# The second modulation and the attention's weights moved behind batch 0's first product, with the written order kept on all engines from there on

## The chip, the cores and the metric

The kernel runs on one core of a Trainium2 chip. The time is device time of one launch in microseconds (us), from the first to the last work of the core. A core has five engines that run side by side, each working through its own queue in order: TensorE (PE in the profile: matrix products and transposes, with PEld for the loading of the stationary operand), VectorE (DVE), ScalarE (ACT), GpSimd (POOL) and SyncE (SP, which here only issues DMA transfers). An instruction that waits for another engine holds back everything that stands behind it in its own queue. So the order in which instructions stand in each queue is part of the kernel.

## What is computed

The reference is a network of two layers on `x` of 8 batches x 512 positions x 128 channels. Each layer has two halves, and before each half the activations are normalised, scaled and shifted by a modulation that is computed from a conditioning vector of the batch:

```python
mod = (silu(c) @ wmod).reshape(8, 6, 1, 128)       # one such mod for each layer
sa, ca, ga, sb, cb, gb = mod[:, 0], ..., mod[:, 5]
ga = (2 * (ga >= 0) - 1) * maximum(abs(ga), 0.25)  # gb likewise
h = layernorm(x) * (1 + ca) + sa
x = x + ga * attn(h)
h = layernorm(x) * (1 + cb) + sb
x = x + gb * ffn(h)
```

In layer 0, `attn` is a recurrence over time (exponentials and running sums of products k, v and r, then a division, then a product with `Wo`), and `ffn` is a linear layer whose inputs and weights are rounded to a 6-bit grid in blocks of 32. In layer 1, `attn` is an attention of 16 heads with three branches (latent keys, 32 chosen positions, window keys), gated and summed, and `ffn` is a gated recurrence over the batches.

## The kernel before

Everything is kept with 128 channels or positions on the partitions and the 512 positions of one batch along the free dimension, in 32-bit floats, so most instructions are 128x512.

Three chains of work are written as Python generators: `layer0()` (for each batch, `layer0_mix` and then `layer0_linear`), `before()` (for each batch, `prepare`, which makes layer 1's inputs) and `recurrence()`. Each `yield` is a place where other work can be put between. The attention's loop (from line 968) walks over 192 units of scores, softmax and weighted sums, and calls `advance`, which takes one step of each chain where the loop leaves room. So while batch b is in the attention, layer 0 of a later batch goes on between the pieces. Before that loop there is nothing to attend to: batch 0 has to go through `layer0_mix`, `layer0_linear`, `prepare` and `group_inputs` first. That stretch is called the start here.

The start is recorded like this. The loads are issued, `modulate(0)` makes layer 0's modulation (line 239; six small products on PE, line 226, called modps, and then small DVE instructions), the mixing weights are scaled (lines 241 to 249), and then

```python
FIRST = 14
for _ in range(FIRST):
    next(stages[0])
remaining()
```

takes 14 steps of `layer0()` and records `remaining()`: the second modulation (`modulate(1)`, line 253), the quantised weight of layer 0's linear half (`mx_quantize` of `fw`, lines 256 to 265, with a transpose on PE called wps), the scaling of the attention's weights on DVE (lines 267 to 276) and the mask on POOL (lines 278 to 281). After that `while (0, 0) not in q_of: next(feed)` and `need("shared", 0)` (lines 955 to 957) record the rest of the start.

The recording is not yet the order in the queues. A scheduler orders the instructions of each engine by what it takes to be urgent, unless they stand inside `tc.manual_schedule(...)`, where the named engines keep the written order. In the kernel before, that region is opened just ahead of the attention's loop (lines 966 and 967), so the start is in the scheduler's order and the attention in the written one.

Names that the change touches, in the order of batch 0's path: `xn` (normalised input, L118), `tp` (its transpose, L126), `h` (L311), products `wkT`, `wvT`, `wrT` (L315, L316), `k` and `v` (L321, L324), `er` (exponential of r, L327), the maximum scan `mx` (L332), `d` and `q` (L335 to L340), their exponentials (L342 to L356), the running sums `aa` (L360, L364) and `bb` (L368), numerator and denominator (L363 to L377), reciprocals (L381), their product `v` (L383), the product `o` with `Wo` (L386), `oT` (L388), the residual (`rp` L131, `x` L133). Then the linear half ends in a second residual, and `prepare` makes `xn1`, `tp1`, `hT` (L442), the latents `cps` and `cq` (L449, L451), their squares and reciprocal roots `ss` and `rr` (L456 to L461, L91 to L96), `tpq` (transposed `cq`), `nqT` (L475), and from it `qR`, `qN`, `k0N`, `k1R` and the first scores `s` (L793). Layer 0 of batch 1 (its `xn`, `tp`, `h`, `wkT` to `wrT`, `k`, `v`, `er`, `mx`, `d`, `q`) is woven into this stretch.

Of the kernel before, what the change touches and what calls it, by code (L numbers as in the profile page):

```python
# [58 lines left out]
def adaln_kernel(ctx: ExitStack, tc: tile.TileContext, x, pa, pb, pc, pt, out):  # L59
    nc = tc.nc  # L60
    V, S, G, PE = nc.vector, nc.scalar, nc.gpsimd, nc.tensor
# [73 lines left out]
    def mx_quantize(dst, src, nb, tmp, key):  # L135

        am = small.tile([128, nb], FP, name=f"am_{key}", tag="am")
        V.tensor_reduce(am, src, AX.X, ALU.max, apply_absolute_value=True)
        yield 0
        sc = small.tile([128, nb], FP, name=f"sc_{key}", tag="sc")  # L140
        V.tensor_scalar(sc, am, 1.0 / 7.5, 1e-30, ALU.mult, ALU.max)
        rc = small.tile([128, nb], FP, name=f"rc_{key}", tag="rc")
        V.reciprocal(rc, sc)
        z = tmp("z")
        V.tensor_tensor(z, src, rc.unsqueeze(2).to_broadcast([128, nb, 32]), ALU.mult)

        yield 0
        e = tmp("e")  # L150
        V.tensor_scalar(e.bitcast(U32), z.bitcast(U32), 0x7F800000, None, ALU.bitwise_and)
        yield 0
        m1 = tmp("m1")
        V.tensor_scalar(m1, e, 1.0, 1.5 * 2.0**20, ALU.max, ALU.mult)
        m2 = tmp("m2")
        V.tensor_scalar(m2, e, 1.0, 1.5 * 2.0**20 + 0.125, ALU.max, ALU.mult)
        q2 = tmp("q2")
        G.tensor_tensor(q2, z, m2, ALU.add)
        yield 0
        q1 = tmp("q1")  # L160
        V.tensor_tensor(q1, z, m1, ALU.add)
        G.tensor_tensor(q2, q2, m2, ALU.subtract)
        yield 0
        V.tensor_tensor(q1, q1, m1, ALU.subtract)
        yield 0
        V.tensor_tensor(q1, q1, q2, ALU.min)
        yield 0
        V.tensor_tensor(dst, q1, sc.unsqueeze(2).to_broadcast([128, nb, 32]), ALU.mult)
# [22 lines left out]
    def bank(shape, name):  # L191
        return ps_t.tile(shape, FP, name=name, tag="t")
# [5 lines left out]
    def part(n, *shape, rows=128):  # L198
        nonlocal taken
        taken += n  # L200
        ap = room[0:rows, taken - n : taken]
        return ap.rearrange("p (a b) -> p a b", b=shape[-1]) if shape else ap
# [13 lines left out]
    def modulate(l):  # L216
        c_in = WA[f"cT{l}"]

        sg = part(B)
        S.activation(sg, c_in, AF.Tanh, scale=0.5)  # L220
        si = sil0 if l == 0 else part(B)
        V.tensor_scalar(sg, sg, 0.5, 0.5, ALU.mult, ALU.add)
        V.tensor_tensor(si, sg, c_in, ALU.mult)
        ps = bank([128, 6, B], f"modps{l}")
        for j in range(6):
            PE.matmul(ps[:, j, :], lhsT=WA[f"wmod{l}"][:, j * 128 : (j + 1) * 128], rhs=si, start=True, stop=True)
        m = mods[l]
        V.tensor_copy(m, ps)
        for j in (1, 4):
            V.tensor_scalar(m[:, j, :], m[:, j, :], 1.0, None, ALU.add)  # L230
        for j in (2, 5):
            sgn = part(B)
            V.tensor_scalar(sgn, m[:, j, :], 0.0, 2.0, ALU.is_ge, ALU.mult)
            mag = part(B)
            V.scalar_tensor_tensor(mag, m[:, j, :], -1.0, m[:, j, :], ALU.mult, ALU.max)
            V.tensor_scalar(mag, mag, 0.25, None, ALU.max)
            V.scalar_tensor_tensor(m[:, j, :], sgn, -1.0, mag, ALU.add, ALU.mult)
# [12 lines left out]

    def remaining():

        modulate(1)


        wq = part(128, 4, 32)
        for _ in mx_quantize(
            wq, WA["fw"].rearrange("p (n k) -> p n k", k=32), 4,
            lambda n: part(128, 4, 32), "w",
        ):  # L260
            pass
        wps = bank([128, 128], "wps")
        PE.transpose(wps, wq.rearrange("p n k -> p (n k)"), ident)
        S.copy(wqT, wps)
        V.tensor_scalar(gbias, mod0[:, 5, :], WA["fbias"], None, ALU.mult)

        qscale = 1.0 / math.sqrt(HD)
        gq = part(1, rows=QL)
        V.tensor_scalar(gq, WB["g"][0:QL, :], qscale, None, ALU.mult)
        V.tensor_scalar(wd[0:QL, :], wd[0:QL, :], gq, None, ALU.mult)  # L270
        V.tensor_scalar(wd[QL:128, 0:512], wd[QL:128, 0:512], WB["g"][QL:128, :], None, ALU.mult)
        V.tensor_scalar(WB["wdk"][0:KVL, :], WB["wdk"][0:KVL, :], WB["g4"][0:KVL, :], None, ALU.mult)
        V.tensor_scalar(WB["wkr"], WB["wkr"], 1.0 / H, None, ALU.mult)

        for n in ("ufT", "uiT", "ucT", "uoT", "bf", "bi"):
            V.tensor_scalar(WC[n], WC[n], 0.5, None, ALU.mult)

        G.memset(mask, 0.0)
        G.affine_select(
            mask, mask, pattern=[[-1, T]], compare_op=ALU.is_ge, fill=NEG, base=T - 128, channel_multiplier=1  # L280
        )
# [603 lines left out]
    def layer0():  # L885
        for b in range(B):
            while b > 3 and ("normed", b - 2) not in ready or b == 1 and ("normed", 0) not in ready:
                yield 0
            yield from layer0_mix(b)
            yield from layer0_linear(b)  # L890
            ready.add(("layer0", b))

    def before():
        for b in range(B):
            while ("layer0", b) not in ready or b > 1 and ("attended", b - 2) not in ready:
                yield 0
            while b > 2 and ("recur", b - 3) not in ready:
                yield 0
            yield from prepare(b)

    def recurrence():
        for b in range(B):
            while ("attended", b) not in ready or (b < B - 2 and ("normed", b + 2) not in ready):
                yield 0
            yield from recur(b)
            ready.add(("recur", b))

    FIRST = 14
    stages = layer0(), before(), recurrence()
    chains = {chain: 0 for chain in stages}  # L910
    for _ in range(FIRST):
        next(stages[0])
    remaining()

    def advance(open_to=TR, of=None):

        for chain in of or list(chains):
            if chains[chain] % M > 0:
                chains[chain] -= 1
            elif chains[chain] in (0, TR, open_to):  # L920
                gap = next(chain, None)
                if gap is None:
                    del chains[chain]
                else:
                    chains[chain] = gap
# [37 lines left out]
    FEEDS = (1, 1, 2, 1, 2, 2)  # L963
    late = []
    projecting = None
    ordered = ExitStack()
    ordered.enter_context(tc.manual_schedule(engines={PE.engine, V.engine, S.engine, G.engine}))
    for i in range(-2, len(units) + 3):
        un = units[i] if 0 <= i < len(units) else None
        ahead = units[i + 2] if i + 2 < len(units) else None  # L970
# [159 lines left out]
```

## Time and profile before

| | before |
|---|---|
| median of 3 runs | 1708.04 us (1707.66 to 1712.55) |
| profiled execution | 1708.48 us, its span 1706.7 us |
| PE busy | 1572.7 us (92% of the span) |
| DVE busy | 1266.0 us (74%) |
| ACT busy | 1152.8 us (68%) |
| POOL busy | 936.8 us (55%) |
| first product of the attention's scores starts | 94.81 us |
| PE busy from 96 us to 1706 us | 1531.83 us of 1610 |
| PE busy from 24 us to 96 us | 27.7 us of 72 |

The table is read in two parts. From 96 us on the PE is busy for 95% of the time, and the instructions of every engine stand in an order that the change leaves as it is. The first 96 us are the start, in which one batch passes from engine to engine, and PE is busy for little more than a third of the time from 24 us on. The column PEclk of the profile gives the clock that TensorE was granted, as a share of full speed: 0.50 means that a product takes about twice as long.

### The profile page before, as it was taken

The numbers are of one execution on the slowest core, as the hardware profiler recorded it, in microseconds if no ns is written. First come the engines' busy times: TensorE is split into PE (matmuls) and PEld (weight loads), VectorE is DVE, ScalarE is ACT, GpSimd is POOL, SyncE is SP. The second block draws the span as 40 slices with busy tenths as digits, with TensorE's granted clock in tenths as the row PEclk, the third lists the DMA queues.
The fourth block names the chain that finished last, engine by engine and source line by source line (L and its number), as shares of the span: only waits on it lengthen the run. The fifth ranks groups of instructions, "written<-read, shape, count | busy, mean of one in ns | idle before, by whom it ended". The sixth has DMA issues, their size and how long they took to land.

```text
span 1706.7 us, 39939 instructions
## 1 busy us (share of the span) xinstructions
PE 1572.7 (92%) x14777; PEld 938.1 (55%) x14777; DVE 1266.0 (74%) x4259; ACT 1152.8 (68%) x3245; POOL 936.8 (55%) x1370
## 2 busy tenths in 40 slices
PE   3388999899999999999899999989999999999997
PEld 2144655465555655655555555655555565665663
DVE  6678878875888868975979768867889667666543
ACT  2244787666776777777666677767776777777882
POOL 2155567554666547554656457654666456655551
PEclk8687999998999999999999999999999999999998
DMA  4000000000000000000000000000000000000012
GB/s 170 1 2 2 2 2 3 7 2 14 3 2 8 7 8 3 1 8 14 3 1 2 7 8 3 2 7 14 3 2 1 14 8 3 1 14 8 14 39 68
DMA packets 13778, 20.55 MB, mean 12 GB/s; under 512 B 912, under 2 KB 9104, under 8 KB 13456
## 3 DMA queue, kind: packets, MB, share of 16 engines
q1 hardware_dynamic: 13584, 17.99, 3.1%
q8 instruction: 118, 1.93, 0.5%
q14 instruction: 76, 0.62, 0.1%
HBM read 11.70 MB, written 5.77 MB: 10 GB/s over the span
## 4 chain that ended last, share of the span: by engine, by line
PE 63%; DVE 26%; ACT 5%; issue 3%; POOL 3%; DMA 0%; POOLq 0%; DVEq 0%; ACTq 0%
PE s L793 19%; PE t L837 12%; DVE p L805 7%; PE o L851 7%; PE s L755 2%; PE k3Rm L638 2%; PE qRm L638 2%; ACT p L814 2%; PE k3Np L610 1%; PE v1p L651 1%; PE op L862 1%; PE o L738 1%; PE qNp L610 1%; ACT pT L603 1%; POOL p L823 1%
## 5 line engine op out<-in xcount | busy, mean ns | idle before, releaser
L823 POOL TENSOR_SCALAR p<-p,rs 128x512 f32<-128x512 f32 (+3 forms) x1024 | 578.8, 586 | 390.9 <-DVE rs L819 221.9
L805 DVE CUSTOM_DVE_ANT_0 p<-s,mask 128x512 f32<-128x512 f32 (+3 forms) x1024 | 442.6, 477 | 178.4 <-PE s L793 178.0
L814 ACT ACTIVATE p<-p,nm 128x512 f32<-128x512 f32 (+3 forms) x1024 | 560.0, 553 | 11.9 <-DVE nm L805 11.8
L603 ACT COPY pT<-t 128x384 f32<-128x384 f32 (+1 forms) x768 | 354.8, 521 | 188.0 <-PE t L837 185.4
L837 PE MATMUL t<-ident,p 128*128 128x128 f32 x2560 | 367.4, 281 | 34.8 <-ACT pT L603 7.2
L837 PEld LDWEIGHTS t<-ident,p 128*128 128x128 f32 x2560 | 276.2, 142 | 160.3 <-issue 115.0
L814 ACT ACTIVATION_READ_ACCUMULATOR p<-p,nm 128x1 f32 x1024 | 197.2, 193 | 0.0
L793 PE MATMUL s<-k3R,qR 32*128 32x128 f32 (+3 forms) x2048 | 188.1, 458 | 4.4 <-DVE nm L805 3.2
L793 PE MATMUL s<-k1R,qR 32*128 32x512 f32 (+3 forms) x2048 | 185.9, 452 | 2.6 <-POOL k1R L625 2.5
L851 PE MATMUL o<-pT,v 128*32 128x512 f32 (+3 forms) x2048 | 153.2, 440 | 0.0
L793 PEld LDWEIGHTS s<-k3R,qR 32*128 32x128 f32 x2048 | 98.8, 188 | 84.4 <-DVE nm L805 30.9
L793 PEld LDWEIGHTS s<-k1R,qR 32*128 32x128 f32 x2048 | 105.4, 186 | 48.5 <-issue 13.6
L851 PEld LDWEIGHTS o<-pT,v 128*32 128x32 f32 x2048 | 60.4, 110 | 111.1 <-issue 100.3
L793 PE MATMUL s<-k0N,qN 32*128 32x512 f32 (+3 forms) x1024 | 102.3, 434 | 0.0
L793 PE MATMUL s<-k3N,qN 32*128 32x512 f32 (+3 forms) x1024 | 96.8, 434 | 0.0
L625 POOL TENSOR_TENSOR k3R<-k3R,rt_k3R 128x512 f32<-128x512 f32 x32 | 40.7, 1272 | 83.9 <-DVE rt_k3R L624 83.9
L805 DVE DVE_READ_ACCUMULATOR2_ANT nm<- 128x1 f32 x1024 | 82.8, 81 | 0.1
L765 POOL TENSOR_TENSOR p<-p,m 128x512 f32<-128x512 f32 x32 | 33.6, 1049 | 67.4 <-DVE m L764 67.4
L638 PE MATMUL qRm<-nqT,wb 96*128 96x512 f32 x128 | 68.8, 621 | 1.2 <-ACT nqT L475 0.7
L793 PEld LDWEIGHTS s<-k0N,qN 32*128 32x128 f32 x1024 | 60.5, 188 | 17.0 <-issue 2.5
L793 PEld LDWEIGHTS s<-k3N,qN 32*128 32x128 f32 x1024 | 55.1, 189 | 22.1 <-issue 15.2
L603 ACT COPY accT<-o 128x512 f32<-128x512 f32 x32 | 18.8, 587 | 71.0 <-PE o L851 71.0
(308 smaller groups left out, 2446.3 us busy)
## 6 DMA issues: line engine op xcount, KB each, us to landing
wb<-pb_dram SPq DMA_DIRECT2D x1, 3731.0 KB, 14.3
x<-x_dram SPq DMA_DIRECT2D x8, 256.0 KB, 3.7
x1all<-x SPq DMA_DIRECT2D x7, 256.0 KB, 2.0
h2all<-h SPq DMA_DIRECT2D x7, 256.0 KB, 2.0
h2o<-h2all SPq DMA_DIRECT2D x7, 256.0 KB, 2.6
x_first<-x1all SPq DMA_DIRECT2D x4, 256.0 KB, 3.6
out_dram<-x_first SPq DMA_DIRECT2D x4, 256.0 KB, 2.2
out_dram<-x SPq DMA_DIRECT2D x4, 256.0 KB, 2.3
```

The source lines that it names most:

```text
L603: S.copy(dst, src)
L610: PE.matmul(ps, lhsT=w[:, g * 128 : (g + 1) * 128], rhs=src, start=True, stop=True)
L625: G.tensor_tensor(lo, lo, r[0], ALU.subtract)
L638: PE.matmul(ps, lhsT=w[:, i * 128 : (i + 1) * 128], rhs=src, start=True, stop=True)
L755: PE.matmul(sp[h][to, :], lhsT=k[js, g, :], rhs=q[js, h * half : (h + 1) * half], start=(i == 0), stop=(i == 2), skip_group_check=True,)
L765: G.tensor_tensor(p2, p2, m2.unsqueeze(2).to_broadcast([128, T // 32, KEEP]), ALU.subtract)
L793: PE.matmul(un.s[j][:, at : at + n], lhsT=q[js, n - 128 : n], rhs=k[js, 0:n], start=(i == 0 and at == 0), stop=(i == 2), skip_group_check= ...
L805: V.tensor_tensor_reduce(out=un.p[:, j, at : at + n], in0=un.s[j][:, at : at + n], in1=mask[:, T - n :], scale=-1.0, scalar=3.4e38, op0=AL ...
L814: S.activation(p, p, AF.Exp, bias=un.nm[:, j, i : i + 1], scale=-1.0, accum_out=un.rs[:, j, i : i + 1])
L823: G.tensor_scalar(p, p, un.rs[:, j, i : i + 1], 1.0, ALU.mult, ALU.mult)
L837: PE.transpose(tp[:, k, :], un.p[:, j, at : at + 128], ident)
L851: PE.matmul(out_ps[js, c * 128 :], lhsT=v[:, c, js], rhs=pT[:, j, at[0] : at[-1] + 1 : step, :], start=not a and c == 0, stop=False, skip_ ...
```

## The change

The second modulation and the scaling of the attention's weights, the recurrent weights and the mask go from `remaining()` into a function of their own, `remaining_later()`. `remaining()` keeps the quantised weight and its bias. The written order begins earlier: the region `tc.manual_schedule` opens before the first steps of `layer0()`. In it, 10 steps are recorded, then `remaining()`, then 21 more steps (up to the product of numerator and reciprocals, just ahead of the product `o`), then `remaining_later()`, and then the rest of the start as before.

```diff
     def remaining():
 
-        modulate(1)
-
 
         wq = part(128, 4, 32)
...
         S.copy(wqT, wps)
         V.tensor_scalar(gbias, mod0[:, 5, :], WA["fbias"], None, ALU.mult)
 
+    def remaining_later():
+
+        modulate(1)
         qscale = 1.0 / math.sqrt(HD)
         gq = part(1, rows=QL)
...
-    FIRST = 14
+    SECOND = 21
+    FIRST = 10
     stages = layer0(), before(), recurrence()
     chains = {chain: 0 for chain in stages}
+    ordered = ExitStack()
+    ordered.enter_context(tc.manual_schedule(engines={PE.engine, V.engine, S.engine, G.engine}))
     for _ in range(FIRST):
         next(stages[0])
     remaining()
+    for _ in range(SECOND):
+        next(stages[0])
+    remaining_later()
...
-    ordered = ExitStack()
-    ordered.enter_context(tc.manual_schedule(engines={PE.engine, V.engine, S.engine, G.engine}))
     for i in range(-2, len(units) + 3):
```

What this does to the queues, read from the two built programs (no times are in this): nothing is added and nothing is taken away. The DMA queue of SP keeps its order. On PE, ACT, POOL and DVE the order differs only ahead of the first softmax of the attention, and from there on it is the same, instruction by instruction. Inside the start:

- PE: wps moves ahead of `wrT`; the six products modps of the second modulation stay directly in front of `o`.
- ACT: `er` moves ahead of the exponentials of batch 0; the tanh of the second modulation moves behind them. For batch 1, `er` and then `nqT`, `qN` and `k0N` stand ahead of its exponentials, which came first before.
- DVE: seven instructions of the quantised weight and of the second modulation's input leave the stretch ahead of `xn`. The second modulation's input (L222, L223) now stands directly behind the product of numerator and reciprocals, and the rest of the modulation and the scaled weights follow it, ahead of the residual `x`. In batch 0's first residual block, L363 moves ahead of the running sum `bb`. In `prepare`, batch 1's normalisation, which alternated with batch 0's one instruction by one, follows it as a block, ahead of `ss`; and batch 1's `mx`, `d` and `q`, which stood inside `rr`, move behind it, with `d` and `q` between the rotations of `qR` and `k1R`.
- POOL: the mask moves behind the numerator of batch 0 (L372); batch 1's `d` moves between the rotations of `qR` and of `k1R`.

## The prediction

> **What bounds the kernel now.** I read the page's engine table and slices first, then the chain of work that ended last for the first 120 us, then the timeline of the same stretch, and last the windows, for the clock. From 96 us on PE is busy for 1531.83 of 1610 us and no queue's order changes there. So the change can only move the moment at which the first scores start, and what it moves goes to the end one to one: behind that moment DVE (37.73 of the 42 us from 96 to 138) and then PE have no gap to take a delay in. The chain of work, time order (start, length, what):
>
> ```profile
> 14.79 2.08 PE wkT L315 x2
> ...
> 23.21 1.24 PE modps L226 x12
> 24.45 0.17 PE wps L263
> 24.62 14.30 issue
> 38.92 2.06 PE o L386 x2
> 41.00 0.70 ACT oT L388
> 41.74 1.13 PE rp L131 x4
> 42.89 0.70 DVE x L133
> ...
> 83.51 0.67 PE tpq L126 x4
> 84.20 0.59 ACT nqT L475
> ...
> 96.03 3.68 PE s L793 x16
> ```
>
> One batch is handed from engine to engine. The "issue" of 14.30 us is no issue: PE's queue holds `o`, which needs DVE's product at 38.13. The timeline shows what ACT, POOL and DVE do meanwhile:
>
> ```profile
> 22.01 0.63 ACT L342 ACTIVATE d<-d 128x512 f32<-128x512 f32 x1
> ...
> 23.77 0.58 ACT L327 ACTIVATE er<-wrT 128x512 f32<-128x512 f32 x1
> ...
> 25.57 1.55 POOL L364 TENSOR_TENSOR aa<-aa,e 128x512 f32<-128x512 f32 x1 [2.13 <-ACT e L351]
> 25.99 1.24 DVE L230 TENSOR_SCALAR mod<-mod 128x8 f32<-128x8 f32 x2
> 26.08 0.63 ACT L356 ACTIVATE q<-q 128x512 f32<-128x512 f32 x1
> 27.14 0.16 DVE L233 TENSOR_SCALAR start<-mod 128x8 f32<-128x8 f32 x1
> ...
> 28.52 1.02 DVE L270 TENSOR_SCALAR wb<-wb,start 96x1536 f32<-96x1536 f32 x1
> ...
> 38.13 0.69 DVE L383 TENSOR_TENSOR v<-v,e 128x512 f32<-128x512 f32 x1
> ```
>
> The second modulation and the weights sit on DVE inside the chain. And two small L230 last 1.24 us, to the end of POOL's L364 at 27.12: DVE stands while POOL reads. The clock, by windows (us, PE busy, ..., granted clock third from the end):
>
> ```profile
> 75.00:75.50 0.50, 0.26 (x2) 0.00 (x0) 0.00 (x0) 0.23 (x2) 0.39 (x1) 0.53 0.00 0
> 85.50:86.00 0.50, 0.50 (x3) 0.18 (x2) 0.00 (x0) 0.00 (x0) 0.00 (x0) 0.72 0.00 0
> 95.50:96.00 0.50, 0.45 (x7) 0.00 (x0) 0.00 (x0) 0.00 (x0) 0.48 (x1) 0.95 0.00 0
> 99.00:99.50 0.50, 0.50 (x4) 0.00 (x0) 0.00 (x0) 0.00 (x0) 0.00 (x0) 0.63 0.00 0
> ```
>
> It flips between half and full about 75.5, 85.7, 96.0 and 99.4, distances of nearly three times, three times and once 3.4 us.
>
> **The change, step by step**, on the clock of the profiled execution (1708.48 us, span 1706.7; 0.44 above the median). No DMA moves, and what is moved needs only loads that have landed by 24 us (the windows show DMA share 0 from there).
>
> 1. Ahead of `xn`: L138 leaves ahead of the first modulation (0.20 from its start to the next), L145 (0.20) and L151 (0.14) behind it. `wkT` starts at 14.79 - 0.5 = 14.3. The quantised weight then runs from 13 to 16, while DVE would wait for `k` until 18 ("DVE mx waited for ACT k", 3.8 us): free, as long as `k` is not earlier than 16.
> 2. PE: 0.5 us earlier at half clock is 0.25 at full clock, wps (0.17 to 0.3) now stands ahead of `wrT`: end 23.1 (23.2 before).
> 3. ACT: `er` stands ahead of the exponentials and waits for `wrT`. Before, `d` started at 22.01; now `er` at 23.1 and `d` at 23.65. From `d` to the end of the last exponential (26.71) it took 4.70 with `er` and wqT inside, some 3.7 without: 27.4 instead of 26.7.
> 4. DVE: L363, now ahead of `bb`, waits for that: 27.4; POOL's L364 (its running sum ends at 26.2) holds until 27.6, as it held L230. L363 ends 28.2, `bb` (1.22) 29.4. Then L371 needs `bb`, DVE has a gap, and POOL's L372 (1.27 alone, as at 120.24) gets in: L371 at 30.7. L551 and L374 to 32.3, L377 to 33.0, four reciprocals (34.64 to 38.13: 3.49) to 36.5. So L383 starts at 36.5 instead of 38.13: 1.6 won of the 3.9 us of modulation and weights that left (L228 0.18, L230 0.14, 27.14 to 30.06, L276 0.67). Without POOL's turn in between it is 35.3; with two DVE operations held as at 30.87 (POOL 3.18 there) 37.1.
> 5. The added wait: L222 and L223 stand behind L383, so modps starts at 36.5 + 0.6 + 0.4 = 37.5. PE is at half clock there (0.50 from 28 to 75), so the twelve take the 2.73 of 8.09, not the 1.24 of 23.21; and `o` stands behind them in PE's queue: 37.5 + 2.64 = 40.1 instead of 38.92, **+1.2**.
> 6. DVE's queue: behind modps (40.25) come the copy, eleven small ones (0.07 apart, 0.20 where one needs the last: 1.5), the weights (L270 0.94, L271 0.44, L272 0.40, L273 0.20) and L276 (0.67): 4.3 us, to 44.6. From `o` to `x` PE and ACT need 3.97 (38.92 to 42.89): 44.1. So this cover is 0.5 too short and `x` waits for DVE's queue, not for `rp`: 44.6, **+1.7**. The mask on POOL (0.53 + 0.61) fits behind L372, long before 96.
> 7. The linear half is unchanged: second residual 64.85 + 1.7 = 66.55.
> 8. `prepare`: batch 0's normalisation is no longer mixed with batch 1's. Residual to `xn1` took 4.97 (64.85 to 69.82); unmixed, the same block at 42.89 to 47.57 took 4.68. `xn1` 71.2, `hT` 72.9 to 73.7. Batch 1's block then starts when DVE is free, at 72.3: sums 1.2, then `hsum` waits for `hT` (73.7 + 0.6), and L91 to L118 take 2.56 (45.01 to 47.57): its `xn` runs 76.9 to 78.0, where it ended at 73.53. Tp and `h` (1.17, 0.79) put `wkT` of batch 1 at 79.4 instead of 76.13: **+3.3**.
> 9. PE's queue again: `tpq` stands behind `wrT` of batch 1. The DVE side improves: `ss` at 78.0, the root without `mx`, `d` and `q` inside 2.6 instead of 5.47 (77.17 to 82.64), `cq` ready at 82.5 instead of 83.45. But the six products end later than that. At full clock they take 5.4 (76.13 to 81.55): 84.8. At the clock of batch 0, whose lead-up is the same (tp, `h`, products, cold), 8.4 (14.79 to 23.21): 87.8. The clock rose 6.1 us into that run; with flips on a grid of 3.4 us it rises between some 2.8 and 6.2 us after the start, so I take 7.5: `tpq` at 86.9 instead of 83.51, **+3.4**.
> 10. `nqT` to the scores: 11.2 before (84.79 to 96.03). DVE's `d` and `q` (0.6 each) and POOL's `d` (1.27) now lie between the rotations; in exchange the products from 85.7 to 89.1, at half clock before, follow a busy stretch and run fast (1.8 us). By the rows I get 10.7 where DVE gets its turn between POOL's instructions and 12.5 where it does not; I take 11.0, **-0.2**.
>
> Sum: scores at 96.03 + 3.2. 1708.48 + 3.2 - 0.44 = **1711.2 us**, 0.19% more. Ends: 35.3 in step 4 (-1.25), full clock in step 9 (-2.1) and 10.7 in step 10 (-0.3) leave -0.4; 37.1 (+0.6), 87.8 (+0.9) and 12.5 (+1.5) give +6.2.
>
> [...]
>
> **The rivals.** *Slower, beyond 0.3%* (5.1 us, about what a measurement of this kernel can tell from no change): PE's queue with the clock. If the six products of batch 1 run at half clock to the end, they take 12 x 0.857 + 0.2 = 10.5, `tpq` comes at 89.9, +6.4, and the time is 1714.2; with step 10 at 12.5 it is 1715.7. It decides from `tpq` at 88.8 on. For it: 76% busy between 13.9 and 17.3 did not raise the clock. Against: it did rise at 20.9 and at 75.5 under such work.
>
> *Nothing arrives*: batch 1's tp gets to PE early enough, the products run at full clock, POOL keeps out of step 4. Then the start is -0.4 to +1: 1707.6 to 1709. For it: DVE has 3.9 us less ahead of `o`. Against: all of step 5 and 6 has to be paid from 1.6 us.
>
> *Faster*: the written order frees the root in step 9 (1 us) and L383 (1.6 to 2.9), and nothing stands behind PE's two queues. Even all together is 3.9 us: 1704. Beyond 0.3% faster it needs scatter as well; the runs before spread over 4.9 us.
>
> **How the numbers follow.** Forecast (+1 to +5.1) 0.50; nothing arrives 0.16; slower beyond 0.3% 0.28; faster 0.06. Within 0.3%: 0.50 + 0.16 = 0.66. The range takes the lower end less a little scatter, 1706.5, and the upper end of the sum plus some, 1715.7; half of the slow rival lies in it.
>
> **What would show it.** In the changed kernel: L383 at 36 to 37 (step 4); modps at half clock, about 2.7 us, directly ahead of `o` at 40 (5); DVE without a gap from modps to `x`, so that the wait of `x` for `rp` (4.1 us before) is gone (6); batch 1's `xn` after `hsum`, `wkT` at 79 (8); `tpq` following `wrT` without a gap, after a wait of POOL's `cq` that costs nothing (9); the first critical score at 99 (10). Wrong I would be if `o` starts before 39, or if `tpq` still follows POOL's `cq` directly: then step 8's delay did not matter and the time is that of before.

## The result and the profile after

The changed kernel took 1717.24 us (median of six, 1716.46 to 1720.29) against 1710.03 us (six, 1707.34 to 1712.84) for the kernel before on the same chip: ratio 1.0049, 95% interval 1.0038 to 1.006. It is 0.49% slower; 1711.2 us had been predicted and the range ended at 1715.7. The profiled execution took 1716.81 us (span 1715.0, mean granted clock 0.955) against 1708.48 (1706.7, 0.960).

The chain of waits of the changed kernel, in order of time (start, length, what), where the prediction showed that of before:

```profile
14.46 2.08 PE wkT L316 x2
...
26.74 10.29 issue
37.03 2.71 PE modps L226 x12
...
44.33 0.61 DVE x L133
...
66.20 0.70 DVE x L133
...
79.97 2.08 PE wkT L316 x2
...
86.54 0.87 PE wrT L317 x2
...
98.24 4.30 PE s L794 x24
```

PE's wait of 14.30 us for batch 0's product is now one of 10.29 us for the inputs of the second modulation. The timeline shows the two places that the change was about, and how the start ends (its bracket: idle time before, and who ended it):

```profile
35.95 0.69 DVE L384 TENSOR_TENSOR v<-v,e 128x512 f32<-128x512 f32 x1
...
37.03 2.70 PE L226 MATMUL modps<-start 128*128 128x8 f32 x12 [14.71 <-issue]
...
39.58 2.06 PE L387 MATMUL o<-v,wb 128*128 128x512 f32 x2
...
42.41 1.11 PE L131 MATMUL rp<-ident,oT 128*128 128x128 f32 x4 [0.78 <-ACT oT L389]
...
43.59 0.74 DVE L277 TENSOR_SCALAR wc<-wc 128x128 f32<-128x128 f32 x6
44.26 0.67 DVE L133 TENSOR_TENSOR x<-rp,x 128x512 f32<-128x512 f32 x1
...
76.24 0.99 DVE L95 TENSOR_TENSOR rt_a<-rt_a,ve_a 128x4 f32<-128x4 f32 x1
...
77.46 1.11 DVE L118 TENSOR_SCALAR xn<-x,mv_a,lrs_a 128x128 f32<-128x128 f32 x4
...
87.23 0.60 PE L126 MATMUL tpq<-ident,cq 128*128 128x128 f32 x4
...
99.46 0.30 PEld L794 LDWEIGHTS s<-k1R,qR 32*128 32x128 f32 x4 [0.71 <-POOL k1R L628]
```

`o` waits for the modulation at half clock, `x` follows DVE's weights without a gap, and batch 1's `xn` ends 5 us later than before. The first product of the scores starts at 98.24 us (94.81 before). The prediction summed up to the products behind POOL's second operation on `k1R`, which start 1.2 us later: 99.46 us, and 96.03 before.

How the delay runs on is seen by laying the 1,024 softmax operations of DVE (line 805 before, 806 changed; the same order in both) beside each other. The difference of their starts, changed less before:

| at (us, before) | 100 | 183 to 390 | 439 | 544 | 600 to 690 | 705 to 760 | 870 to the end |
|---|---|---|---|---|---|---|---|
| changed - before (us) | +2.83 | +2.4, from 340 on +2.1 | +1.95 | +3.6 | +7.2 | +8.95 | +8.6 to 8.8 |

So the start cost 2.8 us, of which 2.0 to 2.4 last until 500 us: what was predicted (+3.2), a little less. Then 6 to 7 us more come between 510 and 710 us, where no queue's order differs. The clock tells when. These are windows of the changed kernel (us, busy time and instructions of PE, PEld, DVE, ACT, POOL, then the granted clock, DMA share, GB/s):

```profile
510.71:514.12 3.41, 1.94 (x10) 1.04 (x11) 3.20 (x17) 3.10 (x9) 2.28 (x4) 1.00 0.00 0
514.12:517.53 3.41, 3.41 (x22) 1.10 (x26) 3.20 (x8) 0.85 (x4) 0.77 (x1) 0.50 0.00 0
...
705.27:708.68 3.41, 1.68 (x16) 1.22 (x16) 3.20 (x16) 1.62 (x4) 3.26 (x9) 1.00 0.00 0
708.68:712.09 3.41, 3.41 (x23) 2.62 (x23) 0.82 (x6) 2.19 (x6) 0.00 (x0) 0.50 0.00 0
```

and the same places of the kernel before:

```profile
508.97:512.38 3.41, 1.96 (x8) 0.91 (x8) 3.17 (x18) 3.10 (x10) 2.23 (x4) 1.00 0.00 0
512.38:515.79 3.41, 3.41 (x59) 2.02 (x58) 3.39 (x7) 0.60 (x2) 1.31 (x2) 1.00 0.00 0
...
696.70:700.10 3.40, 2.55 (x27) 2.03 (x20) 3.26 (x18) 2.15 (x4) 3.40 (x8) 1.00 0.00 0
700.10:703.50 3.40, 2.54 (x28) 2.24 (x32) 2.08 (x10) 1.38 (x3) 1.18 (x3) 1.00 0.00 0
```

At 512 and 706 us PE stands 1.40 and 1.63 us for a bank that `slps` (the transposes of batch 2's and 3's slots) still holds (the pool `ps_t` of L183 has three for PE's products in turn): DVE's copy out of `slps` ends at 513.88 and 708.16, and PE goes on at 513.94 and 708.21. In the changed kernel's execution a step at half clock followed each time: PE got through 22 instructions in 3.41 us instead of 59 (they are not all of one size). A third such stretch, 6.83 us from 596.04, lies between. In the kernel before none of the three is there; near 700 us its bank wait is divided over two steps (2.55 and 2.54 us busy). The changed kernel has 27.3 us at half clock between 500 and 1000 us, before 17.1.

### The profile page after: what moved, and what is told of

Its sections match the earlier page's. It is cut to its first block, busy times and chain, and to the rows that moved or that the text cites. A ratio compares the mean times of both kernels' runs of the same rounds, so it can differ in the third digit from the quotient of the medians.

```text
span 1715.0 us, 39943 instructions
## 1 busy us (share of the span) xinstructions
PE 1577.5 (92%) x14777; PEld 941.4 (55%) x14777; DVE 1270.3 (74%) x4259; ACT 1153.1 (67%) x3245; POOL 938.0 (55%) x1370
## 4 chain that ended last, share of the span: by engine, by line
PE 64%; DVE 25%; ACT 5%; issue 3%; POOL 2%; DMA 0%; POOLq 0%; ACTq 0%; DVEq 0%
PE s L794 20%; PE t L838 12%; PE o L852 7%; DVE p L806 7%; PE k3Rm L639 2%; PE s L756 2%; PE qRm L639 2%; ACT p L815 2%; PE v1p L652 2%; PE op L863 1%; PE o L739 1%; PE k3Np L611 1%; ACT pT L604 1%; PE qNp L611 1%; POOL p L824 1%
```

## Experiments: is it the order, the place, or the execution?

Three theories stood for these 6 us. "One to one": the body only carries the start's delay on, so the 6 us must be the change's own work. "Grid", later "gap in a step": the clock changes in steps of 3.41 us (in the traces of before and of the result every stretch from the first rise on, but for the one that the span's end cuts off, is 3.41 us or a whole multiple), and the place of the body against these steps decides how often it falls to half. "Chance": each execution draws its stretches anew, whatever the kernel.

**Delays alone.** The kernel before, and the changed one, with extra operations on DVE (0.46 us each, one after the other) in front of the products behind POOL's second operation on `k1R`; nothing else moves:

```diff
+    for _ in range(2):                       # 5 in b_delay5, 7 in a_delay7
+        V.tensor_scalar(k1_of[0][:, 1, :], k1_of[0][:, 1, :], 1.0, None, ALU.mult)
     for i in range(-2, len(units) + 3):
```

> The kernel before with two extra, dependent 128x512 operations on DVE ahead of the first scores (some 0.95 us between them), all orders else as before: a pure delay of everything behind 100 us. Theory 'grid' (the body's place against the 3.41-us steps in which the granted clock changes decides whether it falls to half for a step or two at 514, 596 and 708 us): the total is not the delay; it moves by +0.95 us plus or minus the price of one or more half-clock stretches (1.5 to 2 us each), so anything of -2 to +7 us, and the profile shows half-clock stretches at other places than before in 500 to 720 us. Theory 'one to one' (the body only carries the delay on; the other 5 us of the change are made by the change's own instructions): +0.95 us, 1709.4 us for the lower group of its runs, half-clock stretches as before. Theory 'chance' (the stretches come and go from execution to execution whatever the kernel): its runs spread like those of before, the lower group at +0.95 us.

> The same with five such operations, some 2.35 us: about the shift that the change itself made at the first scores (2.83 us at the first softmax, 2.4 us at 180 us). Theory 'grid': the body lands where the change put it, so the half-clock stretches at 514, 596 and 708 us appear here too and the time is 1715 to 1718 us, +7 to +9 us over before. Theory 'one to one': +2.35 us, 1710.8 us for the lower group, no such stretches. Theory 'chance': spread as before, lower group at +2.35 us.

> The changed kernel with the two extra operations on DVE ahead of the first scores (0.95 us). Theory 'grid': the shift against before is then some 3.4 us, one whole step of the clock, so the body stands to the steps as in before: the three stretches can go, and the time can fall to 1711.5 to 1713 us in spite of more work; at the least the half-clock time in 500 to 1000 us changes from 27.3 us. Theory 'one to one': 1716.8 + 0.95 = 1717.8 us with the stretches of the changed kernel. Theory 'chance': 1717.8 us with single runs 3 to 6 us above or below.

| kernel | median (range), us | before on that chip | ratio, 95% interval |
|---|---|---|---|
| before + 2 | 1712.03 (1707.54 to 1719.02) | 1709.5 | 1.0019, 1.0007 to 1.003 |
| before + 5 | 1712.31 (1708.23 to 1717.29) | 1709.5 | 1.0019, 1.001 to 1.0029 |
| changed + 2 | 1712.28 (1709.22 to 1714.98) | 1709.5 | 1.0015, 1.0007 to 1.0024 |

The profile of before + 2 has stretches at 512.1 and 703.3 us, with the instructions of the kernel before from there on: the work of the change is not needed for them.

```profile
508.70:512.12 3.42, 1.96 (x10) 1.06 (x11) 3.21 (x17) 3.11 (x9) 2.27 (x4) 1.00 0.00 0
512.12:515.53 3.41, 3.41 (x22) 1.10 (x25) 3.23 (x8) 0.82 (x4) 0.83 (x1) 0.50 0.00 0
```

The 1.96 us busy are those of the undelayed kernel, in which the clock stayed up. The profile of changed + 2 has none of the three stretches (13.7 us at half clock from 500 to 1000 instead of 27.3). "One to one" falls. But its profiled execution was the slowest of its eleven: it ran at half clock at other places, from 1055.8 us (6.83 us) and from 1291.3 us (3.41 us). And before + 5 spoils a simple rule. "Grid" had it at 1715 to 1718 us; its median was 1712.31, and only the profiled execution, the slowest of twelve, took 1717.29. That one does have stretches at 517.6 and 708.7 us. But its queues are those of before up to 99.97 us, and yet in its profile PE ran at half clock from 87.5 to 108.0 us and the first softmax came 6.42 us later, not 2.35. So the clock differs from execution to execution in the start, too.

**The order and the split alone.** `order_only` opens the written order ahead of the first steps and leaves everything in one piece; `split_only` has the split and the change's counts, but the written order where before has it:

```diff
 # order_only, against before
+    ordered = ExitStack()
+    ordered.enter_context(tc.manual_schedule(engines={PE.engine, V.engine, S.engine, G.engine}))
     for _ in range(FIRST):
...
-    ordered = ExitStack()
-    ordered.enter_context(tc.manual_schedule(engines={PE.engine, V.engine, S.engine, G.engine}))
     for i in range(-2, len(units) + 3):
```

```diff
 # split_only, against the changed kernel
     FIRST = 10
...
-    ordered = ExitStack()
-    ordered.enter_context(tc.manual_schedule(engines={PE.engine, V.engine, S.engine, G.engine}))
     for _ in range(FIRST):
...
+    ordered = ExitStack()
+    ordered.enter_context(tc.manual_schedule(engines={PE.engine, V.engine, S.engine, G.engine}))
     for i in range(-2, len(units) + 3):
```

> The kernel before with the written order taken up already ahead of the first layer-0 steps, and nothing put behind the product: the second modulation and the attention's weights stand in program order, on DVE ahead of batch 0's recurrence. The order of the start alone should then cost more than the whole change did at the start: the second modulation's inputs, its copy, the quantised weight and the attention's weights (some 5 to 8 us of DVE time by their own rows) stand ahead of the first ev, so x at 46 to 49 us against 42.89, the first scores 3 to 6 us later than before. Theory 'one to one': 1711.5 to 1714.5 us for the lower group. Theory 'grid': that plus 0 to 6 us by where it lands.

> The source split and the numbers of steps of the change (10 and 21 instead of 14, the second half called later), but the written order taken up only where before takes it up, so that the scheduler still orders the start. It puts the modulation and the weights back near their old places; all theories: as before, 1708 to 1710 us, first scores within 1 us of before. Were it slower by 5 us or more, the split and not the order would carry the change's loss.

`order_only`: 1717.58 us (1715.45 to 1717.88; before 1709.5), ratio 1.0046, 1.0033 to 1.0059. Its chain:

```profile
34.38 0.61 DVE ev L346
...
46.46 2.06 PE o L386 x2
...
50.43 0.70 DVE x L133
```

`ev` starts at 34.38 (23.56 in the changed kernel), `x` comes 7.5 us later than before and the first softmax 10.2; in its profile none of the three stretches exists and the shift stays at 9.7 us to the end. So at the start the written order by itself costs far more than the change, and putting the modulation and the weights behind the product gives most of that back. In the total its five executions are as slow as those of the result. I had taken 3 to 6 us at the scores: too little. `split_only`: 1708.97 us against 1708.59, ratio 1.0001, 0.9991 to 1.001: no effect of the split is seen.

**The same kernel again.**

> The changed kernel itself, once more, beside the three others. Its first six runs all had a mean clock of 0.955 or 0.956 and 1716.5 to 1720.3 us. Theory 'grid' (the change puts the body at a place against the clock's 3.41-us steps where it falls to half clock more often, whatever the execution): again 1716 to 1720 us at a clock of 0.955 to 0.956 in nearly all runs. Theory 'chance' (each execution draws its stretches anew, and the first six drew badly): a spread as of the kernels with delays, 1709.5 to 1717 us, lower group near 1708 + 2.5 = 1710.5 us at a clock of 0.959 to 0.960.

1716.0 us (1709.46 to 1721.2) against 1708.59, ratio 1.0036, 1.002 to 1.0052: eight of the twelve above 1715 us, as "grid" had it, and four from 1709.46 to 1712.22, as "chance" had it. Its profiled execution took 1710.07 us (clock 0.959). That gives the cleanest comparison of the study: two executions of one kernel, softmax against softmax, first profile less second:

| at (us) | 102 to 490 | 520 | 548 to 576 | 612 to 704 | 739 to the end |
|---|---|---|---|---|---|
| difference (us) | -0.15 to -0.02 | +0.34 | +1.55 | +4.9 to 5.0 | +6.7 to 6.8 |

The second one's windows at the same places:

```profile
510.84:514.26 3.42, 1.95 (x10) 1.06 (x10) 3.19 (x16) 3.10 (x10) 2.27 (x4) 1.00 0.00 0
514.26:517.67 3.41, 3.41 (x58) 1.96 (x57) 3.40 (x7) 0.75 (x3) 1.16 (x1) 1.00 0.00 0
...
702.00:705.41 3.41, 2.17 (x24) 1.96 (x28) 2.41 (x11) 1.27 (x3) 1.55 (x4) 1.00 0.00 0
705.41:708.82 3.41, 3.06 (x27) 1.91 (x19) 1.74 (x6) 3.41 (x12) 0.17 (x1) 1.00 0.00 0
```

The whole 6.74 us between the two executions is made by the three stretches, 1.6 us at 514, 3.4 at 596 and 1.7 at 708. Up to 490 us they agree to 0.15 us. Against the kernel before, this second execution is 2.98 us late at the first softmax and 1.6 at the end.

At 514 us the place against the steps seems to decide, to a tenth of a microsecond: in both, PE is busy for 0.57 of the step with the bank wait, but the step begins at 510.71 us in the first, 0.07 us behind the first transpose of `slps` (510.64), and at 510.85 in the second, 0.17 us behind it (510.68). Over the fourteen profiles without the filling product of the next experiment, the three in which the clock fell here have 0.07, 0.08 and 0.10 us, the eleven in which it stayed 0.17 to 0.40. And one stretch goes with the next: in the first execution the bank wait near 706 us comes 5.0 us later, one whole step and 1.6 us, and falls whole into one step (1.68 us busy), where in the second it is divided (2.17 and 3.06). In all three profiles with a stretch at the wait of batch 2 there is one at the wait of batch 3, and in none of the other eleven. Why the clock fell at 596 us is open.

**A step more, and the gap filled.** `a_delay7` adds almost one whole step (3.3 us). `after_fill` gives PE something to do in the two bank waits:

```diff
-        slps = bank([128, NC], f"slps_{b}")
+        slps = bank([128, T], f"slps_{b}")
         for c in range(NC):
             PE.transpose(slps[:, c : c + 1], ...)
+        if b in (2, 3):
+            PE.matmul(slps[:, 128:T], lhsT=ident, rhs=WB["wselk"][:, 0:384], start=True, stop=True)
...
-        V.tensor_copy(slT, slps)
+        V.tensor_copy(slT, slps[:, 0:NC])
```

> The changed kernel with two extra matrix products (128x384, some 0.64 us each, results never read) on PE behind slps of batch 2 (510 us) and of batch 3 (705 us), where PE otherwise stands 1.40 and 1.63 us for a bank. The profiles so far: a 3.41-us step in which PE is busy for less than 0.51 of it was followed by a step at half clock in all 119 cases, with 0.60 to 0.65 in none of 36; these two places have 0.57 and, when the gap falls whole into one step, 0.49. Theory 'gap in a step' (the extra half-clock stretches come from PE's gap at the batch boundaries falling into one step of the clock, and the change only moves the body so that it does): with the gaps filled to 0.75 no stretch at 514 and 708 us in any execution, so more work on PE makes the kernel faster: median 1710 to 1712 us instead of 1716 to 1717, no group of runs at a clock of 0.955. Theory 'the change's own work': as the changed kernel, 1716 to 1717 us. Theory 'chance': as the changed kernel's second twelve, 1709.5 to 1721 us, spread in two groups.

> The changed kernel with seven of the extra DVE operations ahead of the first scores, 3.3 us, nearly one whole step of the clock (3.41 us). Two of them (0.95 us) had made the kernel faster, 1712.3 us median with no run below a clock of 0.958. Theory 'gap in a step': with a whole step more the body stands to the steps as in the changed kernel itself, so the group of runs at 0.955 to 0.957 is back, and the median is 1716.5 + 3.3 = 1719 to 1720.5 us: +3.3 to the changed kernel, but +7 to the one with two operations. Theory 'one to one': 1712.3 + 2.35 = 1714.7 us.

`a_delay7`: 1718.21 us (1712.33 to 1721.66; before 1709.41), 1.0048, 1.0033 to 1.0064. Five operations more than in changed + 2 are 2.3 us, and the median was 5.9 us higher (six executions, on another chip, with the same time for before), nearer to "gap in a step" (1719 to 1720.5) than to "one to one" (1714.7). Yet its profile has none of the three stretches; it lost its time at half clock from 95.8 to 106.1 and from 119.7 to 126.6 us (3.41 us each in the changed kernel) and in a step at 789 us. `after_fill`: 1713.3 us (1710.24 to 1716.57), 1.0027, 1.0017 to 1.0038, above the 1710 to 1712 that "gap in a step" had. In its profile the waits are filled, and the clock stayed:

```profile
511.02:514.43 3.41, 2.56 (x12) 1.40 (x12) 3.19 (x16) 2.50 (x8) 2.27 (x4) 1.00 0.00 0
514.43:517.85 3.42, 3.42 (x58) 1.98 (x57) 3.40 (x7) 1.35 (x4) 1.15 (x1) 1.00 0.00 0
...
705.60:709.02 3.42, 3.41 (x30) 2.22 (x22) 2.10 (x8) 3.42 (x12) 0.53 (x1) 1.00 0.00 0
```

These runs were on different chips, so the three kernels were then put on one:

> The changed kernel once more, now on one chip with the filled and the delayed one, as the yardstick for both. All theories: median 1715 to 1717.5 us, most runs at a clock of 0.955 to 0.957 (14 of 18 so far).

> The filled kernel (one 128x384 product behind slps of batches 2 and 3) beside the changed kernel on the same chip. 'Gap in a step': median 2.5 to 5 us below the changed kernel's, no stretch that begins at 512 to 519 or 700 to 710 us in its profile; what remains above 1710.5 us comes from stretches elsewhere. 'The change's own work' and 'chance': the same median as the changed kernel within 1 us, or up to 1.3 us more (the two products).

> The changed kernel with two extra DVE operations (0.95 us) beside the changed kernel on the same chip. 'Gap in a step': median 3 to 5 us below the changed kernel's, hardly a run at or below a clock of 0.957 (0 of 11 so far). 'One to one' and 'chance': 0.95 us above it.

| kernel | median (range), us; before 1709.36 | ratio, 95% interval |
|---|---|---|
| changed | 1711.22 (1708.63 to 1713.3) | 1.0012, 1.0003 to 1.0021 |
| changed, filled | 1711.62 (1709.27 to 1716.43) | 1.0019, 1.0009 to 1.003 |
| changed + 2 | 1710.27 (1709.67 to 1715.37) | 1.001, 1.0002 to 1.0019 |

All three expectations failed here, because the changed kernel itself had no execution above 1713.3 us this time. Filled, it was not faster; two of its eleven executions were still above 1716 us. The two bank waits are therefore not the whole of it. With two operations more its median is 0.95 us lower, which the intervals do not tell from no difference.

All executions, by the sets that were run together on one chip, counted as late (a limit that was set after the runs) when they are more than 5 us above 1707.5 us (the lower group of before) plus the delay of the kernel's start (2.3 us for the change, 0.95, 2.35 or 3.3 more for the added operations):

| kernel | the result's runs | 2nd set | 3rd set | 4th set | 5th set | together |
|---|---|---|---|---|---|---|
| before | 2 of 6 | 2 of 29 | 3 of 35 | 0 of 21 | 1 of 32 | 8 of 123 |
| before + 2 | | 3 of 12 | | | | 3 of 12 |
| before + 5 | | 1 of 12 | | | | 1 of 12 |
| changed | 6 of 6 | | 8 of 12 | | 0 of 11 | 14 of 29 |
| changed + 2 | | 0 of 11 | | | 0 of 11 | 0 of 22 |
| changed + 7 | | | | 4 of 6 | | 4 of 6 |
| changed, filled | | | | 2 of 9 | 2 of 11 | 4 of 20 |

So neither theory alone holds. Whether an execution is late is not fixed by the kernel (one kernel, 1709.5 and 1721.2 us), and the share of late ones changes from set to set. But it does not depend on the execution alone: in the two sets in which the changed kernel was late at all, it was so in 6 of 6 and 8 of 12 executions, and the kernel before beside it in 2 of 6 and 3 of 35. That 0.95 us of delay lowers the share (none of 22) is not shown: in the one set where changed and changed + 2 ran side by side, neither was ever late. What sets the share is open. Of the executions that were not profiled only the mean granted clock is on record, and it fits: 0.955 to 0.957 in the 14 late ones of the changed kernel, 0.957 to 0.961 in the other 15.

**Steps 5 and 9 by themselves.** `a_mod_early` puts the second modulation's inputs and product back behind `wrT`; its copy, small operations and the weights stay behind the product:

```diff
-    remaining()
-    for _ in range(SECOND):
+    si1 = remaining()                        # ends with sg, si of the second modulation
+    next(stages[0])                          # wrT, er
+    ps1 = modulate_ps(1, si1)                # its twelve products
+    for _ in range(SECOND - 1):
         next(stages[0])
-    remaining_later()
+    remaining_later(ps1)
```

> The changed kernel with the second modulation's inputs and its product put back behind wrT; only its copy, the eleven small operations and the attention's weights stay behind the product of batch 0. By the chain of the changed kernel o then starts at 36.6 instead of 39.58 us, DVE's queue behind the product ends at some 41 us and the sum x at 41 instead of 44.26: -3.3 us to the changed kernel up to the first scores, which come at 96.2 instead of 99.46. Theory 'one to one' and 'chance': 1713.9 less the rest, that is the lower group at 1707 to 1708 us and single runs up to 4 us above. Theory 'grid': some place against the steps like that of before (3.3 us is nearly one whole step), 1707 to 1712 us.

1710.41 us (1708.59 to 1713.28; before 1708.59), 1.0014, 1.0005 to 1.0022.

```profile
36.97 0.69 DVE v L391
...
42.14 0.61 DVE x L133
...
96.41 3.98 PE s L801 x17
```

The first scores come at 96.41, 1.83 us before those of the changed kernel (98.24). I had written 3.3: 96.2 instead of 99.46 for the products behind POOL's second operation, which came at 97.63. `x` was expected at 41 and came at 42.14: with the wait for modps gone, DVE's queue behind the product (4.5 us from 37.66) is what `x` waits for. Steps 5 and 6 cannot be added: they are two bounds on the same `x`.

`early_norm` goes on from there and takes batch 1 off the way to `tpq`:

```diff
+        if b == 0:                           # behind the quantised input of the linear half
+            early.append(work("l0", [128, NC, D], "xn0_1"))
+            for _ in ln_norm("a1", (early[0], 1)):
+                pass
         yield TR + G1
```

Batch 1's tp, `wkT` and `wvT` then follow the second residual at once, and `wrT` stands behind `cps`.

> Beyond a_mod_early: the normalisation of batch 1 is taken up while DVE waits for the linear half of batch 0 (59 to 65 us), its products wkT and wvT stand on PE ahead of tp of xn1, wrT behind cps, and the scan, d and q ahead of the sums of squares. Then tpq waits for nothing of batch 1: x at 41 us, second residual at 63, hT at 69.5, cq at 76.5 and tpq at 76 to 78 us against 83.51 before and 87.23 changed, scores at 89 to 91 us. Theory 'one to one' and 'chance': -5 to -6.5 us to before, 1701.5 to 1703.5 us in the lower group. Theory 'grid': that plus 0 to 6 us by where the body lands.

1710.12 us (1705.4 to 1717.05), 1.0017, 1.0003 to 1.0031; the first scores came at 97.73, those of the expectation at 98.95 instead of 89 to 91. `tpq` did come earlier, at 82.61. But look at the products behind it:

```profile
82.61 1.13 PE tpq L126 x4
...
84.40 3.78 PE qRm L662 x4
...
91.89 3.73 PE k1Rm L662 x4
...
97.73 5.54 PE s L817 x24
```

```profile
72.76:76.18 3.42, 2.84 (x12) 1.53 (x12) 3.39 (x4) 1.07 (x2) 1.51 (x2) 1.00 0.00 0
76.18:79.59 3.41, 0.00 (x0) 0.00 (x0) 2.06 (x8) 1.85 (x4) 1.66 (x2) 1.00 0.00 0
79.59:83.00 3.41, 0.39 (x2) 0.39 (x3) 2.97 (x13) 0.00 (x0) 0.78 (x1) 0.50 0.00 0
```

PE had nothing from 76.18 to 79.59, the clock fell, and everything to the scores ran at half (0.50 from 84.40 to 97.60 us too). Batch 1's products, which step 9 had counted as an obstacle to `tpq`, may then also be what keeps the clock up for what follows. `warm_norm` puts them back between `cps` and `tpq`, keeps the early normalisation, and moves the weights behind `hsum`:

```diff
         V.tensor_reduce(hsum, hT, AX.X, ALU.add)
+        if b == 0:
+            weights()                        # out of remaining_later
...
+        for _ in range(14 if b == 1 else 0): # ahead of batch 1's wkT
+            yield M
```

> As early_norm, but batch 1's six products stand on PE between cps and tpq (72 to 81 us), so that PE is busy ahead of tpq and the clock has risen when the products behind it run; the attention's weights stand on DVE behind hsum, where it waits for the squares (72 to 74.6 us), instead of ahead of x. In early_norm the products of batch 1 ran at 65 to 71 us, the clock fell back to half at 79.6 us, and everything from tpq to the scores took 13.2 us at half clock (84.4 to 97.6) against 8.2 to 9 in the others. If the clock ahead of tpq is the matter: x at 41.8, second residual at 63.6, tpq at 80 to 82 us, the products behind it at full clock, scores at 92 to 94 us against 96.03 before; 1704 to 1707 us in the lower group, plus the stretches of the body. If the clock does not rise in time: scores at 96 to 97, 1708 to 1710 us.

1706.11 us (1702.99 to 1710.13) against 1709.41, ratio 0.9984, 0.9975 to 0.9992.

```profile
42.25 0.70 DVE x L133
...
80.59 0.68 PE tpq L126 x4
81.29 0.59 ACT nqT L499
...
81.92 1.98 PE qRm L662 x4
...
85.82 1.07 PE k1Rm L662 x2
...
90.80 4.33 PE s L817 x24
```

The scores of the expectation come at 92.02, where 92 to 94 was expected. `tpq` is 2.0 us earlier than in `early_norm`, the scores 6.9. What lies between is the clock: the twelve products from `qRm` to `k1Rm` keep PE busy for 11.2 us there, at half clock, and for 5.8 us here, at full clock (1.00 in all windows from 76.67 to 90.30 us). It is faster than the kernel before, which the changed kernel was in none of its three sets. With the two fills:

> warm_norm (second modulation's product early, batch 1's normalisation early and its products between cps and tpq, weights behind hsum) with the two filling products behind slps of batches 2 and 3. Its own scores at 90.8 us stay. If the filled gaps matter there too: the median falls from 1706.1 to 1703.5 to 1705.5 us, and no run above 1709. If warm_norm's place already keeps the gaps apart: the same within 1 us, 1705.5 to 1707 us.

1704.06 us (1701.99 to 1709.18) against 1709.36, ratio 0.9973, 0.9961 to 0.9984. The intervals of the two overlap, so that the fills add anything is not shown.

## Why the prediction was wrong, point by point

| step | predicted | profile of the changed kernel |
|---|---|---|
| 1, 2: `wkT`; end of `wrT` | 14.3; 23.1 | 14.46; 22.33 |
| 3: last exponential's end | 27.4 | 26.63 |
| 4: last product on DVE | 36.5 | 35.95, POOL got its turn as assumed |
| 5: modps; `o` | 37.5; 40.1 (+1.2) | 37.03; 39.58 (+0.66) |
| 6: `x`, by DVE's queue | 44.6 (+1.7) | 44.26 (+1.37); `rp` ended at 43.5 |
| 7: second residual | 66.55 | 66.20 |
| 8: `xn1`; batch 1's `wkT` | 71.2; 79.4 (+3.3) | 70.88; 79.97 (+3.84) |
| 9: six products; `tpq` | 7.5; 86.9 (+3.4) | 7.4; 87.23 (+3.72) |
| 10: end of `nqT` to the critical scores; sum | 11.0; +3.2 | 10.9 (88.58 to 99.46); +3.4 |

Each step of the start held to 0.8 us, and the wait for modps, the queue on DVE and batch 1's late `xn` are where they were put. Rows 2 to 7 came 0.3 to 0.8 us early: the clock rose 4.7 us after batch 0's `wkT` started (at 19.19), and 6.1 us after it before. Row 8 lost that again, by a DVE operation of 0.16 us that took 0.99 while POOL squared (the `rt_a` line above, POOL's L457, 1.04 us from 76.17; its neighbours on DVE took 0.16). In step 9 the clock rose at 84.04, 4.1 us after `wkT` started; batch 0 before had needed 6.1, and I had taken a value below that. That the sum is met to 0.2 us is partly luck: in two more profiles of the same kernel the first scores came 3.6 and 4.4 us later than before, not 3.4.

The step that failed is the sentence ahead of them: "what it moves goes to the end one to one". It was true in one direction, since the body has no gap that takes the delay in: +2.83 became +2.0 to 2.4. But the sum lacked a term, the half-clock stretches of the body. They cost 6 us in the profile on record and nothing in the next profile of the same kernel (+1.6 us to before at its end); between these two executions lie 13.65 us at half clock and 6.7 us of time. I had read the clock's grid in the start and priced it there, and the rival for "slower" was that same clock in step 9; I did not ask what it does in the 1,600 us behind. The runs shown had the hint: the kernel before varied by 4.9 us from execution to execution, and I took that as scatter of the measurement.

By the median of 29 executions in three sets the changed kernel takes 1713.3 us, the kernel before (123 executions) 1709.4. The start's cost is shown: 2.8 to 4.0 us at the first softmax in three profiles, of which 1.8 and 3.0 are left at the last one in the two profiles without the stretches. The rest is a share of late executions that was 6 of 6 in one set and 0 of 11 in another.

## What to carry to other kernels

A few microseconds at the start of a kernel that is bound by PE afterwards are cheap to forecast from the chain, step by step; whether the body behind keeps its clock is not, and belongs into the range as a term of its own, read from the spread of the clock over the executions. Two executions of one kernel, laid beside each other operation by operation, show in one look what the clock makes of it. And independent products ahead of a dependent chain can be worth their time: with them between `cps` and `tpq` the scores came 6.9 us earlier than without, and `tpq` itself only 2.0.

## What the runs showed of the hardware that I had not expected

In all 17 profiles the granted clock changes in steps of 3.41 us (stretches of 3.41, 6.83, 10.24, 17.07 us and other whole multiples), and the steps stand elsewhere against the start in each execution (the first rise is at 20.86 us before and at 19.19 in the result's). I took PE's busy share of every step at full clock, from the first rise of the clock to the end of the span, and the clock in the next one. These are counts of these executions, not a rule for others:

| PE busy in the step | steps | followed by half clock |
|---|---|---|
| under 0.51 | 222 | 220 |
| 0.51 to 0.60 | 66 | 12 |
| 0.60 to 0.70 | 92 | 1 |
| 0.70 to 0.90 | 571 | 12 |
| over 0.90 | 6748 | 0 |

In the traces of before and of the result alone, half clock followed in 29 of 29 steps under 0.51, 1 of 7 from 0.51 to 0.60, 0 of 10 from 0.60 to 0.70, 3 of 66 from 0.70 to 0.90 and 0 of 794 over 0.90.

From half clock it came back behind none of the 372 steps that were under 0.80 busy, 11 of 42 from 0.80 to 0.85, and 13 of 17 from 0.85 to 0.90. Over 0.95 it came back behind 212 of 256, the others mostly in one place at 390 us, where the clock stays down for three steps; why is open. At `slps` of batch 2 all fourteen unfilled profiles have 0.57: three fell, eleven did not. So this share alone does not tell them apart; what divides the two groups is where the step begins (0.07 to 0.10 us behind the first transpose of `slps`, or 0.17 to 0.40). Why that matters at the same share is open.

In microseconds: the step with one idle piece of PE of 1.63 us (1.68 us busy of 3.41) was followed by half clock at 708.68 us; the one with 1.40 us (1.94 busy) was at 514.12 too, but at this place that was so in three of fourteen profiles only.
